# Moving a third of layer two's own-row projections from the second pass over the edges to the first, in a graph layer with a mixture of experts behind it

## The chip, the cores and the metric

The kernel runs on one core of a Trainium2 chip. The metric is the device time of one execution in microseconds; the times shown are the median, the lowest and the highest of several runs. A core has five engines with instruction streams of their own: TensorE (PE, with PEld for its weight loads), VectorE (DVE), ScalarE (ACT), GpSimd (POOL) and SyncE (SP, which here only issues DMAs). They meet through semaphores.

## The reference

The input is `x` (6250 x 512, f32) and 100000 edges `src`, `dst`, sorted by `dst`. Two graph layers run on the normalised rows, then a mixture of experts:

```python
def _sage_layer(h, src, dst, W_self, W_neigh, b, n_nodes):
    agg = segment_sum(h[src], dst, num_segments=n_nodes)
    deg = segment_sum(ones_like(dst), dst, num_segments=n_nodes)
    h_neigh = agg / maximum(deg, 1.0)[:, None]
    return relu(h @ W_self + h_neigh @ W_neigh + b)
...
h = _sage_layer(layernorm(x), src, dst, W_self1, W_neigh1, b1, n)
h = _sage_layer(h, src, dst, W_self2, W_neigh2, b2, n)
x = x + h
x = x + moe(layernorm(x))    # 8 experts, the best 2 of each row
```

All weights of the graph layers are 512 x 512. What matters here is layer two: it needs, of each row of layer one's result h1, the *neighbour part* h1 @ W_neigh2 (summed over the edges later) and the *own part* h1 @ W_self2 + b2. The own part is what the change moves.

## The kernel before

The rows form 49 tiles of 128 (the last has 106). After a first stage (normalising), two passes over the edges follow, both written by the helper `sums` (from L200), then a stage for the experts that is left over.

**A pass.** The edges are cut into 782 lists of 128. A pass has 197 steps; a step takes four lists. For every list GpSimd issues one indirect DMA that gathers 128 rows of 2 KB (L220) into a buffer of a ring: 16 buffers in the first pass (tile `rows_t`), 12 in the second (parts of `big`). VectorE builds one-hot masks for a step (L230, `hot`) two steps ahead. PE multiplies masks and gathered rows into a strip of sums (L248, tile `pa`, eight instructions a step). GpSimd's gathers run three steps ahead of PE in the first pass and two in the second; a gather must wait until PE has used up the buffer that it writes, which is that of four steps earlier in the first pass and three in the second. Three steps make a group: after each group the strip is rounded into three bf16 parts (L258, L272 to L274). When all groups of a tile of rows are there, `take_out` (L283) multiplies them with a selection (L290) and so gets the tile's sums. Tile 8 is taken out in step 40, tile 9 in step 43, tile 10 in step 49; this pattern, three tiles in twelve steps, goes on: for tile b with b mod 3 = 2 the next tile follows three steps later and the one after that six steps later.

**The first pass** ("first sums") calls `layer1` (L552) for each tile that is taken out. It schedules the tile's work in later steps, as (steps behind, place in the step, function):

- u0 (+1, "post", tiles below 36 only): the tile's own part of layer one, xn @ W_self1 (L559), with a bias add (L564);
- u1 (+1, "mid"): the sums are transposed (L194, evicted at L196);
- u2 (+2): times W_neigh1 (L559), then scaled and added to the own part by VectorE (L573, tile `h`);
- u3 (+3): h is transposed, with the relu in the eviction (L196), and for tiles below NS = 36 stored to DRAM as `h1T` (L578);
- u4 (+4): times W_neigh2, copied by ScalarE into part b of `big` (L584) and stored to `z2` (L585);
- u5 (+5, "post", tiles 36 to 44): times W_self2 (L559), bias add (L591), stored to `s2` (L592). For tiles 45 to 48 it is done after the pass.

"mid" is between the step's L248 matmuls and the closing of a group, "post" is at the step's end. A projection (L559) is four f32 matmuls of 128x512, which the profile shows as eight instructions. `big` (49 parts of 128x512) holds in turn each tile's transposed rows, its own part of layer one, and the z2 and s2 rows that are being stored; behind the stores, every fourth tile, SyncE loads 1 MB of the experts' first weights W1 into parts 0 to 31 (L609). W_self2, its bias and two padded copies of the edge lists are loaded from ScalarE's queue when tile 18 is taken out (L597 to L600).

**The second pass** ("second sums") gathers from `z2`. Beside its steps, `each` (L1021) gives out work. In three of every four steps, from step 1 to step 47, it calls `share_of(q)` (L921): tile q's h1T, which SyncE has fetched into a slot of three (L919), times W_self2 (L925, eight instructions), bias add (L927), store to `s2` (L928), and the fetch for tile q + 3. So the own parts of tiles 0 to 35 are made here: the "shares". `route` (L946), called for each tile that is taken out, adds the own part (fetched from s2 one tile ahead, L943) and the neighbour part (L1005), normalises, finds the experts and sends the rows to them by two indirect DMAs (L993). From about step 60 on, each even step also starts a tile of experts' work (L814 to L886). W2 is loaded by 1 MB in eight of the tiles (L640).

**The order.** In both passes the instructions of PE, DVE, ACT and POOL stand in the order in which the program writes them (`manual_schedule`); only SyncE's DMAs are ordered by the framework. All queues are worked in order: what stands behind a waiting instruction of the same engine waits too.

Of the kernel before, what the change touches and what calls it, by code (L numbers as in the profile page):

```python
# [39 lines left out]
P = 128  # L40
# [9 lines left out]
def bcast(ap, n):  # L50

    return bass.AP(tensor=ap.tensor, offset=ap.offset, ap=[[0, P], [1, n]])
# [15 lines left out]
def gnn_moe(ctx, tc, x, src, dst, Ws1, Wn1, gb1, Ws2, Wn2, gb2, Wg, W1, b1, W2, b2, gamma, beta, out):  # L68
    nc = tc.nc
# [7 lines left out]
    NB = (N + P - 1) // P  # L77
# [11 lines left out]
    s2 = dram.tile([N, D], F32, name="s2")  # L89
# [100 lines left out]
    def transposed(pool, psp, t, func, n=P, out=None, bufs=2):  # L190

        pt = psp.tile([P, C, P], F32, name="pt")
        for c in range(C):
            nc.tensor.transpose(pt[:, c, :n], t[:n, c * P : (c + 1) * P], ident[:n, :n])  # L194
        tT = pool.tile([P, C, P], F32, name="tT", bufs=bufs) if out is None else out
        nc.scalar.activation(tT[:, :, :n], pt[:, :, :n], func)  # L196
        return tT
# [128 lines left out]
    def part(i):  # L326
        return big[:, i * D : (i + 1) * D]
# [87 lines left out]
    NS = 3 * NB // 4  # L415
# [124 lines left out]
    lay = b_ctx.enter_context(tc.tile_pool(name="lay2", bufs=1, side="left"))  # L540
    wn2, ws2 = (lay.tile([P, C, D], F32, name=name) for name in ("wn2", "ws2"))
    bb2 = lay.tile([P, D], F32, name="bb2")
    h1T = dram.tile([NS, P, D], F32, name="h1T")

    with tc.tile_pool(name="s1", bufs=2, side="right") as pool, \
            tc.tile_pool(name="s1a", bufs=1, space=PSUM) as pap, \
            tc.tile_pool(name="s1p", bufs=2, space=PSUM) as psp:

        LATE = 4
        late = []  # L550

        def layer1(b, pa, pd):  # L552
            n = rows[b]
            r = slice(b * P, b * P + n)
            own = {}

            def project(ph, tT, w, start, stop):
                for c in range(C):
                    nc.tensor.matmul(ph, tT[:, c], w[:, c], start=(start and c == 0), stop=(stop and c == C - 1))  # L559

            def u0():
                ps = psp.tile([P, D], F32, name="pm")
                project(ps, xnT[b], ws1, True, True)
                nc.vector.tensor_add(part(b), ps, bb1)  # L564

            def u1():
                own["aT"] = transposed(pool, psp, own["a"], AF.Copy)

            def u2():
                ph = psp.tile([P, D], F32, name="pm")  # L570
                project(ph, own["aT"], wn1, True, True)
                own["h"] = pool.tile([P, D], F32, name="h", bufs=1)
                nc.vector.scalar_tensor_tensor(own["h"], ph, rcnt[:, b : b + 1], part(b), op0=OP.mult, op1=OP.add)  # L573

            def u3():
                own["hT"] = transposed(pool, psp, own["h"], AF.Relu, out=xnT[b] if b >= NB - LATE else None)
                if b < NS:
                    nc.sync.dma_start(h1T[b], own["hT"].rearrange("p c n -> p (c n)"))  # L578

            def u4():  # L580
                pz = psp.tile([P, D], F32, name="pm")
                project(pz, own["hT"], wn2, True, True)
                t = part(b if b < NB - LATE else b - LATE)
                nc.scalar.copy(t, pz)  # L584
                nc.sync.dma_start(z2[r], t[:n])  # L585

            def u5():
                ps = psp.tile([P, D], F32, name="pm")
                project(ps, own["hT"], ws2, True, True)
                t = part(b - 1 if b < NB - LATE else b)  # L590
                nc.vector.tensor_add(t, ps, bb2)  # L591
                nc.sync.dma_start(s2[r], t[:n])  # L592

            if b == 0:
                nc.scalar.dma_start(wn2, Wn2.rearrange("(c p) f -> p c f", p=P))
            if b == NS // 2:
                nc.scalar.dma_start(ws2, Ws2.rearrange("(c p) f -> p c f", p=P))  # L597
                nc.scalar.dma_start(bb2, bcast(gb2, D))
                nc.scalar.dma_start(dpad[:E], dst)
                nc.scalar.dma_start(spad[:E], src)  # L600
            nc.vector.tensor_reduce(deg[:, b : b + 1], pd[:, 0 : NDEG : NDEG // 2], AX.X, OP.add)
            nc.vector.tensor_scalar(rcnt[:, b : b + 1], deg[:, b : b + 1], 1.0, None, op0=OP.max)
            nc.vector.reciprocal(rcnt[:, b : b + 1], rcnt[:, b : b + 1])
            own["a"] = pool.tile([P, D], F32, name="a", bufs=1)
            nc.scalar.copy(own["a"], pa)
            e = (b - 5) // 4
            if b >= 5 and (b - 5) % 4 == 0 and e < NE:

                nc.sync.dma_start(w1[:, e * KD : (e + 1) * KD].rearrange("p (c h) -> p c h", c=C),  # L609
                                  W1[e].rearrange("(c p) h -> p c h", p=P))  # L610
            if b >= NB - LATE:
                late.append(u5)
            return ([(1, "post", u0)] if b < NS else []) + [
                (1, "mid", u1), (2, "mid", u2), (3, "mid", u3), (4, "mid", u4)
            ] + ([(5, "post", u5)] if NS <= b < NB - LATE else [])

        with tc.manual_schedule(engines=HAND):
            sums(xn_d, pool, pap, lambda: pap.tile([P, D], F32, name="ps"),
                 pap.tile([P, 2, NDEG], F32, name="pn"), layer1,
                 lambda: pool.tile([P, D], F32, name="rows_t", bufs=16), 16)  # L620
            for u5 in late:
                u5()
# [274 lines left out]
    def fetch_hidden(k):  # L897
        nc.sync.dma_start(part(NW + k % NE), hd[rest[k]])

    with tc.tile_pool(name="s2", bufs=2, side="right") as pool, \  # L900
# [13 lines left out]
        shares = {}  # L914

        def fetch_h1(q):
            if q < NS:
                shares[q] = w2[:, (21 + q % 3) * D : (22 + q % 3) * D]
                nc.sync.dma_start(shares[q], h1T[q])  # L919

        def share_of(q):  # L921
            hT = shares.pop(q).rearrange("p (c n) -> p c n", c=C)
            ps = psp.tile([P, D], F32, name="ph")
            for c in range(C):
                nc.tensor.matmul(ps, hT[:, c], ws2[:, c], start=(c == 0), stop=(c == C - 1))  # L925
            t = w2[:, (24 + q % 2) * D : (25 + q % 2) * D]
            nc.vector.tensor_add(t, ps, bb2)  # L927
            nc.sync.dma_start(s2[q * P : (q + 1) * P], t)  # L928
            fetch_h1(q + 3)
            if q == 0:  # L930
                fetch_own(0)
# [5 lines left out]
        def fetch_own(b):  # L937
            if b < NB:
                n = rows[b]
                xa = pool.tile([P, D], F32, name="xa")  # L940
                nc.sync.dma_start(xa[:n], x[b * P : b * P + n])
                sa = part(NW + 12)
                nc.sync.dma_start(sa[:n], s2[b * P : b * P + n])  # L943
                own[b] = xa, sa
# [76 lines left out]
        def each(i):  # L1021


            at_slot[0] = i
            if i == last_slot + 1:
                for k in range(EARLY):
                    fetch_hidden(k)
            q = i - 1 - i // 4
            if i % 4 and q < NS:
                return [(0, "post", lambda: share_of(q))]  # L1030
            j = up_next[0]
            if i % 2 or j >= upto_n[-1]:
                return []
            c = max(c for c in range(len(n0)) if n0[c] <= j)
            if ready.get(c, 1 << 30) > i:
                return []
            up_next[0] += 1
            u = Up(j, pool, psp, keep=j not in soon)
            todo = [(1, "post", u.fetch), (3, "mid", u.turn_x), (5, "mid", u.times), (6, "mid", u.turn_h)]
            if j in soon:  # L1040
                d = {}

                def begin():
                    d[0] = Down(j, u.hT, u.e, pool, psp, pool.tile([P, D], F32, name="y", bufs=1))
                    d[0].rows = {"gamma": "ph", "beta": "ph"}
                    d[0].times()

                todo += [(8, "mid", begin), (8, "post", lambda: d[0].spread()), (9, "mid", lambda: d[0].scale()),
                         (10, "post", lambda: (d[0].affine(), d[0].finish()))]
            return todo  # L1050

        for q in range(3):
            fetch_h1(q)
        with tc.manual_schedule(engines=HAND):
            sums(z2, pool, pap, lambda: psp.tile([P, D], F32, name="ph"), None, route, ring, 12, each)
# [316 lines left out]
```

## Time and profile before

| | us |
|---|---|
| median of 3 runs | 3350.38 |
| lowest, highest | 3343.76, 3356.97 |
| the profiled execution's own time | 3328.7 |
| its span, first to last instruction | 3326.4 |
| mean granted PE clock | 0.894 |
| first sums, first to last gather's matmul (L248, `rows_t`) | 121.3 to 1294.5 |
| second sums, the same (`big`) | 1336.2 to 2760.3 |
| shares (L925), first to last | 1354.6 to 1656.1 |

| engine | busy us | share of the span |
|---|---|---|
| PE | 2694.6 | 81% |
| POOL | 1846.9 | 56% |
| DVE | 1346.4 | 40% |
| ACT | 691.5 | 21% |

A line of a group reads: source line, engine, operation, what it writes <- what it reads, size, count | busy time, mean duration of one in ns | idle time of the engine just before, and what ended most of it. "issue" is time in which the engine waited for nothing that the profile shows, "remote" a semaphore whose sender is not found. PE's ends are modelled, its starts are measured. Busy shares are means over stages with different limits, and so the text goes by stage.

### The profile page before, as it was taken

To read this page: it belongs to the slowest core of one execution; us is meant where nothing else is said; L and a number is where in the kernel's file an instruction comes from. 1 tells how busy PE (TensorE), PEld (TensorE's weight loads), DVE (VectorE), ACT (ScalarE), POOL (GpSimd) and SP (SyncE) were. 2 spreads that over 40 slices of the span, in tenths; PEclk is the share of its full clock that TensorE was granted. 3 is DMA by queue.
4 is the path that set the end of the run, shared out by engine and by line. 5 is a ranking of instruction groups with operands and counts; after the bars stand their busy time and mean duration, and the time that the engine had idled before them with its cause. 6 is when DMAs were issued, how large, how long until landed. Compare 5 with 4: busy or idle time off the path is not lost. (4 is left out here: it accounts for less than half of the span.)

```text
span 3326.4 us, 34415 instructions
## 1 busy us (share of the span) xinstructions
PE 2694.6 (81%) x10010; PEld 1075.8 (32%) x10010; DVE 1346.4 (40%) x4313; ACT 691.5 (21%) x1261; POOL 1846.9 (56%) x2129
## 2 busy tenths in 40 slices
PE   6768878788887789778747888887888888899995
PEld 3223323233332333223212333332333333344442
DVE  6422222222222222234334454445445454654675
ACT  2211111111111111011112222232222322122221
POOL 4466666666666662666666555555655551650443
PEclk8988988988989899889868888997988998999997
DMA  7767667766776663888877667776766663321696
GB/s 234 229 193 211 205 205 211 226 208 206 217 210 207 198 200 107 268 270 283 269 237 259 220 206 218 221 221 210 222 206 209 216 219 109 129 73 57 217 305 226
DMA packets 266654, 693.41 MB, mean 208 GB/s; under 512 B 42684, under 2 KB 42798, under 8 KB 266428
## 3 DMA queue, kind: packets, MB, share of 16 engines
q0 software_dynamic: 144000, 464.43, 46.4%
q1 hardware_dynamic: 118796, 219.84, 19.2%
q10 hardware_dynamic: 3664, 6.85, 0.6%
q8 instruction: 85, 1.39, 0.2%
q14 instruction: 109, 0.89, 0.1%
HBM read 554.35 MB, written 137.40 MB: 208 GB/s over the span
## 5 line engine op out<-in xcount | busy, mean ns | idle before, releaser
L220 POOL DMA_INDIRECT big<-z,srcT x782 | 748.9, 958 | 584.2 <-PE pa L248 241.8
L220 POOL DMA_INDIRECT rows_t<-xn_d,srcT x782 | 740.5, 947 | 470.2 <-issue 187.5
L559 PE MATMUL pm<-wn,tT 128*128 128x512 f32 x752 | 365.9, 631 | 46.7 <-ACT tT L196 29.1
L826 PE MATMUL ph<-big,xg 128*128 x544 | 312.8, 727 | 79.1 <-DVE y L884 50.1
L860 PE MATMUL py<-w,hT 128*128 x656 | 306.7, 611 | 13.0 <-ACT y L878 8.5
L248 PE MATMUL pa<-big,hot 128*32 128x512 f32 x1564 | 252.0, 662 | 9.9 <-DMA big<-z,srcT 5.9
L248 PE MATMUL pa<-rows_t,hot 128*32 128x512 f32 x1564 | 238.8, 621 | 12.4 <-DMA rows_t<-xn_d,srcT 9.6
L1095 POOL DMA_INDIRECT big<-ys,yrow x98 | 106.9, 1090 | 230.6 <-DMA ys<-y 135.0
L559 PEld LDWEIGHTS pm<-wn,tT 128*128 128x128 f32 x752 | 142.2, 199 | 275.2 <-issue 214.8
L826 PEld LDWEIGHTS ph<-big,xg 128*128 128x128 f32 x544 | 121.5, 235 | 281.2 <-issue 214.2
L290 PE MATMUL ps<-st,sel 128*128 128x512 bf16 (+1 forms) x459 | 139.1, 450 | 47.7 <-issue 38.7
L860 PEld LDWEIGHTS py<-w,hT 128*128 128x128 f32 x656 | 119.3, 192 | 177.9 <-issue 135.9
L925 PE MATMUL ph<-w 128*128 128x512 f32 x288 | 148.8, 665 | 23.4 <-DVE big L1005 17.3
L559 PE MATMUL pm<-ws,big 128*128 128x512 f32 x320 | 153.9, 627 | 0.0
L993 POOL DMA_INDIRECT xs<-big,slot x98 | 98.6, 1006 | 98.1 <-DVE slot L989 43.1
L273 ACT CAST st<-pa 128x512 bf16<-128x512 f32 x132 | 77.3, 586 | 344.3 <-DVE pa L272 211.8
L265 DVE CAST counts<-pn 128x8 bf16<-128x8 f32 x66 | 10.9, 166 | 340.4 <-remote 177.0
L837 DVE TENSOR_SCALAR hT<-pt,b1T 128x128 f32<-128x128 f32 x272 | 76.7, 343 | 177.6 <-PE pt L834 133.0
L290 PEld LDWEIGHTS <-sel 128*128 128x128 bf16 (+1 forms) x918 | 85.7, 107 | 189.9 <-issue 96.5
L1005 DVE SCALAR_TENSOR_TENSOR big<-ph,rcnt,big 128x512 f32<-128x512 f32 (+1 forms) x49 | 36.8, 751 | 266.1 <-PE ph L290 94.0
L1136 PE MATMUL ph<-big,xg 128*128 x296 | 136.9, 605 | 0.0
L290 PE MATMUL ph<-st,sel 128*128 128x512 bf16 (+1 forms) x459 | 120.1, 411 | 17.5 <-DVE sel L280 14.6
(265 smaller groups left out, 3473.8 us busy)
## 6 DMA issues: line engine op xcount, KB each, us to landing
xg<-xs SPq DMA_DIRECT2D x105, 256.0 KB
ys<-y SPq DMA_DIRECT2D x105, 256.0 KB
rows_t<-xn_d,srcT POOLq DMA_INDIRECT x782
big<-z,srcT POOLq DMA_INDIRECT x782
z<-big SPq DMA_DIRECT2D x48, 256.0 KB
xa<-in_x SPq DMA_DIRECT2D x48, 256.0 KB
big<-s SPq DMA_DIRECT2D x48, 256.0 KB
accs<-xa SPq DMA_DIRECT2D x48, 256.0 KB
```

Source lines behind the costliest of these rows:

```text
L220: nc.gpsimd.indirect_dma_start(out=gathered[t], out_offset=None, in_=z[:, :], in_offset=bass.IndirectOffsetOnAxis(ap=srcT[:, t : t + 1], a ...
L248: nc.tensor.matmul(pa[0][q * SW : (q + 1) * SW], hots[i][:, q], gathered.pop(t), start=(j == 0), stop=(j == TS - 1 or t == NT_E - 1), tile ...
L273: nc.scalar.copy(st[1][:k], pa[:k])
L290: nc.tensor.matmul(ps, sel[:k], st[h][:k], start=(g == a and h == 0), stop=(g == z and h == 2))
L559: nc.tensor.matmul(ph, tT[:, c], w[:, c], start=(start and c == 0), stop=(stop and c == C - 1))
L826: nc.tensor.matmul(ph, self.xT[:, c], w1[:, bass.ds(self.e * KD + c * D, D)], start=(c == 0), stop=(c == C - 1))
L837: nc.vector.tensor_scalar(hT[:, c], pt[:, c], b1T[:, bass.ds(self.e * HC + c, 1)], 0.0, op0=OP.add, op1=OP.max)
L860: nc.tensor.matmul(self.py, self.hT[:, c], w2[:, bass.ds(self.e * KD + c * D, D)], start=(c == 0), stop=False)
L925: nc.tensor.matmul(ps, hT[:, c], ws2[:, c], start=(c == 0), stop=(c == C - 1))
L993: inst = nc.gpsimd.indirect_dma_start(out=xs[:, :], out_offset=bass.IndirectOffsetOnAxis(ap=slot[:n, b, k : k + 1], axis=0), in_=t["xn"][: ...
L1095: nc.gpsimd.indirect_dma_start(out=yk[:n], out_offset=None, in_=ys[: ready[0] * P, :], in_offset=bass.IndirectOffsetOnAxis(ap=yrow[:n, b, ...
L1136: nc.tensor.matmul(ph, u.xT[:, c], w1[:, bass.ds(u.e * KD + c * D, D)], start=(c == 0), stop=(c == C - 1))
```

## The change

The list `later` holds the tiles whose own part stays in the second sums: all below 6, and of 6 to 35 those whose number modulo 3 is not 2. The ten others (8, 11, ..., 35) get a u5 in the first sums, like the tiles 36 to 44, and no `h1T` store. Their s2 rows go through part b of `big`, where the z2 rows of the same tile were a step before; tiles from 36 on use part b - 1 as they did. W_self2 and what is loaded with it is loaded when tile 3 is taken out, not tile 18. In the second sums 26 shares are left, one in every odd step from 1 to 51.

```diff
+    later = [b for b in range(NS) if b < 6 or b % 3 != 2]
...
                 own["hT"] = transposed(pool, psp, own["h"], AF.Relu, out=xnT[b] if b >= NB - LATE else None)
-                if b < NS:
+                if b in later:
                     nc.sync.dma_start(h1T[b], own["hT"].rearrange("p c n -> p (c n)"))
...
                 project(ps, own["hT"], ws2, True, True)
-                t = part(b - 1 if b < NB - LATE else b)
+                t = part(b - 1 if NS <= b < NB - LATE else b)
                 nc.vector.tensor_add(t, ps, bb2)
                 nc.sync.dma_start(s2[r], t[:n])
...
-            if b == NS // 2:
+            if b == 3:
                 nc.scalar.dma_start(ws2, Ws2.rearrange("(c p) f -> p c f", p=P))
...
-            ] + ([(5, "post", u5)] if NS <= b < NB - LATE else [])
+            ] + ([(5, "post", u5)] if b < NB - LATE and b not in later else [])
...
         def fetch_h1(q):
-            if q < NS:
+            if q < len(later):
                 shares[q] = w2[:, (21 + q % 3) * D : (22 + q % 3) * D]
-                nc.sync.dma_start(shares[q], h1T[q])
+                nc.sync.dma_start(shares[q], h1T[later[q]])
...
-            nc.sync.dma_start(s2[q * P : (q + 1) * P], t)
+            nc.sync.dma_start(s2[later[q] * P : (later[q] + 1) * P], t)
...
-            q = i - 1 - i // 4
-            if i % 4 and q < NS:
+            q = i // 2
+            if i % 2 and q < len(later):
                 return [(0, "post", lambda: share_of(q))]
```

In the changed kernel the lines from L547 on stand two lines lower.

## The prediction

> **What bounds the kernel now.** I read the windows view first, one stretch for each stage, then the costliest groups of the page, then GpSimd's waits in the same stretches, and last the timeline of a few steps around the place where work is added. The windows (length, busy time and instructions of PE, PEld, DVE, ACT, POOL, then granted clock, DMA share, GB/s):
>
> ```profile
> 121.00:1276.00 1155.00, 924.81 (x3643) 346.66 (x3643) 285.89 (x880) 173.10 (x308) 735.20 (x778) 0.90 0.70 207
> 1336.00:1656.00 320.00, 247.97 (x900) 89.77 (x900) 113.45 (x374) 43.85 (x82) 207.14 (x233) 0.87 0.83 274
> 1656.00:1735.00 79.00, 42.85 (x182) 12.86 (x181) 25.35 (x91) 12.66 (x22) 54.10 (x62) 0.67 0.75 248
> ```
>
> The first row is the first sums, the second is the part of the second sums that holds the 36 shares, the third is the same sums just after the last share. In the first sums PE is busy 80% (924.81 of 1155). The groups give the unit prices:
>
> ```profile
> L220 POOL DMA_INDIRECT rows_t<-xn_d,srcT x782 | 740.5, 947 | 470.2 <-issue 187.5
> L559 PE MATMUL pm<-wn,tT 128*128 128x512 f32 x752 | 365.9, 631 | 46.7 <-ACT tT L196 29.1
> L925 PE MATMUL ph<-w 128*128 128x512 f32 x288 | 148.8, 665 | 23.4 <-DVE big L1005 17.3
> ```
>
> GpSimd issues a gather in 0.95 us and then pauses 0.30 us, so four gathers, one step, take at least 5.0 us, and 197 steps 985 us of the 1155. The rest is waiting. GpSimd's waits in the first sums (us, times, longest):
>
> ```profile
> POOL rows_t L220 <- issue: 186.9, 566, 4.8
> POOL rows_t L220 <- remote: 101.2, 83, 3.5
> POOL rows_t L220 <- PE pa L248: 98.1, 60, 4.6
> ```
>
> The first line is mostly the 0.30 us pauses; all other lines together are 233 us, 20% of the stage, and they are waits for PE to give a ring buffer back. So two things bound a step: GpSimd's 5.0 us, and PE's lateness. Where PE is late is seen by taking the first L248 matmul of every step as the step's start. Steps 37 to 156 repeat in twelves (three tiles in each), and the means of ten repeats, by step number modulo twelve, are, as duration / PE idle in it: 1: 8.1/3.1; 2: 8.7/2.8; 3: 5.2/0.4; 4: 9.1/4.2; 5: 8.7/0; 6: 5.4/0.6; 7: 3.6/0; 8: 8.8/0.4; 9: 5.4/0.6; 10: 1.6/0; 11: 6.5/1.4; 0: 0.9/0. The sum is 71.9 us, 6.0 a step, with 13.4 us of PE idle. From 5 to 10 PE works without a pause and GpSimd waits for it; at 1, 2 and 4 PE waits for ScalarE and VectorE, which wait for PE's own signals, that arrive late ("remote").
>
> The place of the change is step 9 (45, 57, ...). PE and POOL lines of steps 45 and 46:
>
> ```profile
> 409.09 1.06 PE L248 MATMUL pa<-rows_t,hot 128*32 128x512 f32 x8
> ...
> 410.09 3.70 PE L559 MATMUL pm<-wn,tT 128*128 128x512 f32 x8
> 410.41 0.94 POOL L220 DMA_INDIRECT rows_t<-xn_d,srcT  x1 [0.59 <-PE pa L248]
> ...
> 413.72 1.06 PE L248 MATMUL pa<-rows_t,hot 128*32 128x512 f32 x8
> ...
> 416.51 0.94 POOL L220 DMA_INDIRECT rows_t<-xn_d,srcT  x1 [1.40 <-PE pt L194]
> ```
>
> Step 45's matmuls end at 410.15 and the gather for step 49, which takes their buffers, starts 0.26 us later; the gather for step 50 likewise follows the matmuls of step 46. Over the ten repeats the gathers that use the buffers of step 9 start 0.4 us, and of step 10 0.7 us, after the matmuls' ends. GpSimd hangs on PE exactly here.
>
> **The change, part by part.** *Ten projections come into the first sums* (tiles 8, 11, ..., 35). The order of PE's instructions puts each between the u2 of the next tile and the L248 of step 10: in the timeline between the eight that start at 410.09 and the L248 at 413.72. One is eight instructions; at full clock eight take 3.70 us (410.09), and by the group 365.9/752 x 8 = 3.9 us. The L248 of step 10 moves back by 3.9 us, and with it the gather that follows it by 0.7 us, where the shortest such distance seen is 0.2; so 3.9 - 0.5 = 3.4 us are felt by GpSimd each time, 34 us in ten. Some comes back: steps 10, 11 and 0 are PE's lightest, and steps 1, 2 and 4 hold 10.1 us of PE idle. But this idle ends with signals that come when GpSimd has stopped and its transfers have drained, and GpSimd is what has been delayed; so I count a fifth as absorbed: **+27 us**. Bounds: 0 (all of it fits into the 13.4 us of idle) and 54 (ten at the 5.40 us that eight such instructions take at 753.85, after a pause).
>
> *VectorE* gets ten bias adds. The same kind of add takes 0.69 us (L564), 7 us in all, in an engine that is 25% busy. The add stands behind the h of the next tile (L573), so that chain is not held up; behind it stand the next one-hot masks (414.49), which wait until the projection ends, some 3.9 us later. They are for steps 48 and 49, and step 48 starts at 420.9, with the projection's delay on top. Nothing, while signals come in time; rival three prices the rest. The add also writes the buffer that tile's z2 row block is being stored from: a new wait for a DMA. That store is issued at 405.83 and the add could start at 417.4 at the earliest; the longest wait for such a store that SyncE's own waits show is 3.5 us, so 11.6 us cover it.
>
> *DMAs:* ten s2 stores take the place of ten h1T stores, 256 KB each, in the same stage; no byte more. In SyncE's queue each stands behind its tile's z2 store and ahead of the next tile's h1T store, and some W1 loads go behind an h1T store; W1 is used only in the second sums. The loads of Ws2, the bias and the two padded edge lists move from tile 18 to tile 3 in ScalarE's queue: 2.1 MB in the same stage, some 25 steps before the first use. Nothing.
>
> *Ten shares leave the second sums.* 80 PE instructions, 148.8/288 x 80 = 41 us of PE time, ten adds, ten loads and ten stores, 5.2 MB. What that brings is set by what bounds those steps. By the same step starts, steps 2 to 47 with three shares in four take 291.7 us, 6.48 each; steps 52 to 64, without any share, take 78.2 us, 6.52 each, though PE is busy 54% there instead of 77%. GpSimd's waits other than for issue are 59.6 of 320 us with shares and 13.1 of 79 us after, 18.6 and 16.6%. If the two points tell of a share's cost, 36 shares are worth 320 x (1 - 0.814/0.834) = 8 us at most, ten about 2. The stretch after the shares holds three W2 loads of 1 MB in twelve steps, more than the stretch before, so it flatters the shares; I take **-4 us**. Bounds: 0, and -41 (all of PE's time); the bytes alone, at the row's 274 GB/s, are 19 us.
>
> *Half the steps instead of three in four*, up to step 51 instead of 47: the last two shares now lie in steps 49 and 51, whose PE idle (2.3 and 7.8 us) takes most of them in. No tile's s2 is needed earlier than it comes: tile 9's is made in step 17 and read after step 40.
>
> The granted clock is 0.87 with shares and 0.67 without, and eight instructions take 3.70 us in a busy stretch and 5.40 us after a pause. The Trainium skill, TensorE: Matmul & The Clock Gate, Part 1: The HAM clock gate, states the rule behind such rows, that an idle window of about 3.4 us halves the clock until a busy one has passed; it speaks against the change, since the thinned steps leave PE idle more often, and it would charge the 26 remaining shares up to 26 x 1.7 = 44 us of PE time (an estimate) where the sum above charges none, because PE does not set those steps.
>
> **Sum:** +27 - 4 = +23 us. The profiled execution took 3328.7 us (span 3326.4), so that it would take 3351.7; the median of the runs shown is 3350.4, 21.7 us above the profiled one, so that I forecast **3373 us** for the median.
>
> **Rivals.** *One, no difference:* the 3.9 us disappear in the idle of steps 1, 2 and 4. For it: 10.1 us of idle stand there in every twelve steps, and an additional wait of GpSimd lets transfers drain, and so PE's late signals through, earlier. Against it: the gather hangs on L248 within 0.7 us. +6 - 4: 3352.
>
> *Two, faster:* shares are dearer in the second sums than in the first, because DMA is at 0.83 there against 0.70 and PE idles after them in stalls of 10 us and more (8.8 in step 14, 11.5 in step 38). If a stall goes with every third share that leaves, ten times 4.1 us of PE time or the 19 us of bytes come back: between the two -30, with +6 for the first sums, -24: 3326. Against it: 6.48 and 6.52 us a step.
>
> *Three, clearly slower:* VectorE, held at the new add by a late signal, builds masks too late, and PE waits for them. VectorE's waits for remote signals reach 14.6 and 26.0 us in this stage (deg and counts); if every new add waits 5 us past the masks' due time, that is 10 x 5 = 50 more: 3423. It decides from the point where the signal is over 7 us late (from 417.4 to 420.9 + 3.9).
>
> That the change doesn't do what it says can be left aside: the instruction order shows ten projections more in the first sums and ten shares fewer in the second.
>
> **How the numbers follow.** The forecast has 0.52, one 0.27, two 0.13, three 0.08. Under 0.5%, 17 us, a measurement of this kernel can't tell a change from none. The forecast's own range is +10 to +38; an eighth of it lies within 17 us. Slower: 0.52 x 0.88 + 0.08 = 0.54; faster: nearly all of two, 0.12; same: the rest, 0.34. The range leaves out half of two and most of three: 3332 to 3396.
>
> **What would show it.** Right: the step starts of the first sums show step 9 longer by 3.7 to 4 us, GpSimd's wait ahead of the gathers for step 2 grown by some 3 us, and the stage longer by 20 to 35 us; the second sums up to step 52 shorter by under 10 us. Wrong, by rival one: step 9 longer but step 1 or 2 shorter by as much. By two: the share stretch shorter by 20 us or more. By three: VectorE's wait at the new add over 7 us, and PE waiting for hot masks, which it hardly does now. The steps after 64 should not change at all.

## The result, and the profile after

| | before | after |
|---|---|---|
| median of 5 runs, us | 3350.38 | 3380.28 |
| lowest, highest | 3343.76, 3359.7 | 3376.29, 3389.74 |
| the profiled execution's own time | 3328.7 | 3380.28 |
| its span | 3326.4 | 3378.0 |

The ratio is 1.0104, with a 95% interval of 1.0073 to 1.0136: slower by 30 us at the median. The two profiles lie further apart, 51.6 us of span, because the one of before is 21.7 us under its median and the one of after is the median.

Where the 51.6 us are follows from the first L248 of each step: first gather's matmul +2.5 us; first sums 1173.1 -> 1207.5, +34.4 (steps 37 to 157: 722.4 -> 766.6, +44.2; the rest -9.8); between the passes 41.7 both; second sums to step 52 342.6 -> 349.6, +7.0, steps 52 to 64 -7.2, the rest +4.1; what comes after the passes +10.8, with the same work in both (in the profiles of the later runs this part takes 573 to 581 us with either kernel; 566.1 and 576.9 here). So most of the loss, 34.4 us, is in the first sums, and the second sums gave nothing back. There, steps 2 to 47 fell from 291.7 to 285.0 us, but steps 47 to 52, into which the last two shares were moved, grew from 26.5 to 37.6.

The same 120 steps (37 to 157) and the share stretch to step 52, by the windows view of before (length, busy time and instructions of PE, PEld, DVE, ACT, POOL, granted clock, DMA share, GB/s):

```profile
349.00:1072.00 723.00, 589.31 (x2368) 226.48 (x2364) 185.77 (x577) 114.13 (x203) 457.64 (x484) 0.90 0.70 211
...
1336.00:1679.00 343.00, 259.50 (x956) 93.00 (x959) 121.25 (x399) 46.02 (x85) 223.53 (x251) 0.87 0.82 270
```

and of after:

```profile
348.00:1115.00 767.00, 615.81 (x2418) 242.29 (x2440) 190.43 (x579) 112.52 (x201) 457.77 (x484) 0.90 0.66 196
...
1373.00:1723.00 350.00, 249.45 (x865) 84.86 (x879) 116.21 (x392) 47.52 (x88) 227.12 (x256) 0.83 0.78 254
```

In the first row PE gains 26.5 us of busy time (some matmul records of after are missing) and GpSimd none, but the stretch is 44 us longer, and DMA falls from 211 to 196 GB/s: the engines wait more. In the second row PE does 10 us less and DMA is less busy, and still the stretch is 7 us longer: the busy time of neither bound it.

The place of the change, steps 45 and 46, in the timeline of after:

```profile
406.30 1.07 PE L248 MATMUL pa<-rows_t,hot 128*32 128x512 f32 x8
...
408.15 3.70 PE L561 MATMUL pm<-wn,tT 128*128 128x512 f32 x8 [0.78 <-ACT tT L196]
...
411.69 3.60 PE L561 MATMUL pm<-ws,tT 128*128 128x512 f32 x8
411.89 0.75 DVE L575 SCALAR_TENSOR_TENSOR h<-pm,rcnt,big 128x512 f32<-128x512 f32 x1 [0.71 <-PE pm L561]
415.21 1.07 PE L248 MATMUL pa<-rows_t,hot 128*32 128x512 f32 x8
415.32 0.69 DVE L593 TENSOR_TENSOR big<-pm,bb 128x512 f32<-128x512 f32 x1 [2.68 <-PE pm L561]
...
418.01 0.95 POOL L220 DMA_INDIRECT rows_t<-xn_d,srcT  x1 [5.69 <-PE pa L248]
```

The added eight (411.69) stand between u2 and the L248 of step 46, which starts 8.9 us after that of step 45, not 4.6; and GpSimd stands for 5.69 us before it gathers for step 50. Over ten repeats of twelve steps, step 9 grew from 5.4 to 8.1 us, the wait ahead of the gathers for step 2 from 0.2 to 3.0 us, and the twelve steps from 71.9 to 76.3 us. (Such sums of twelve, the prediction's and all below, leave out step 156, the last of the stretch; with it the 120 steps give 72.2 and 76.7.) Steps 1, 2 and 4, whose PE idle was 3.1, 2.8 and 4.2 us, now have 0.7, 11.2 and 0.6: three stalls have become one long one.

What ends that long stall is ScalarE's copy of the taken-out sums, which by the program waits for a signal from PE. ScalarE's waits at this copy, in before:

```profile
ACT a L605 <- remote: 130.0, 17, 16.0
```

and in after:

```profile
ACT a L607 <- remote: 252.3, 29, 16.1
```

17 and 29 of 49 copies wait for a signal whose sender is not found, up to 16 us, long after PE's record of the matmuls. From the start of the last matmul of a take-out (L290) to this copy the median is 2.6 us in before and 4.2 us in after, the longest 14.2 and 14.5.

### The profile page after: what moved, and what is told of

Read it like the earlier page. It is cut to its first block, busy times and chain, and to the rows that moved or that the text cites. A ratio compares the mean times of both kernels' runs of the same rounds, so it can differ in the third digit from the quotient of the medians.

```text
span 3378.0 us, 34248 instructions
## 1 busy us (share of the span) xinstructions
PE 2702.9 (80%) x9914; PEld 1083.4 (32%) x10010; DVE 1347.7 (40%) x4313; ACT 690.1 (20%) x1261; POOL 1846.1 (55%) x2129
## 5 line engine op out<-in xcount | busy, mean ns | idle before, releaser
L248 PE MATMUL pa<-big,hot 128*32 128x512 f32 x1564 | 276.4, 671 | 31.1 <-issue 15.7
L248 PE MATMUL pa<-rows_t,hot 128*32 128x512 f32 x1564 | 241.4, 616 | 12.8 <-DMA rows_t<-xn_d,srcT 9.7
L194 PE MATMUL pt<-ident,a 128*128 128x128 f32 x196 | 36.6, 318 | 164.1 <-ACT a L607 136.1
L561 PE MATMUL pm<-ws,big 128*128 128x512 f32 x320 | 167.3, 673 | 0.0
L603 DVE TENSOR_REDUCE deg<-pn 128x1 f32<-128x2 f32 x49 | 7.8, 159 | 352.8 <-remote 274.9
L274 DVE TENSOR_TENSOR st<-pa,st 128x512 bf16<-128x512 f32 x132 | 91.2, 691 | 89.0 <-ACT st L273 47.8
L290 PEld LDWEIGHTS <-sel 128*128 128x128 bf16 (+1 forms) x918 | 80.6, 101 | 140.1 <-issue 57.7
L290 PE MATMUL ps<-st,sel 128*128 128x512 bf16 x411 | 106.8, 397 | 21.7 <-issue 19.7
```

What stands on the lines that cost most here:

```text
L248: nc.tensor.matmul(pa[0][q * SW : (q + 1) * SW], hots[i][:, q], gathered.pop(t), start=(j == 0), stop=(j == TS - 1 or t == NT_E - 1), tile ...
L274: nc.vector.tensor_sub(st[2][:k], pa[:k], st[1][:k])
L290: nc.tensor.matmul(ps, sel[:k], st[h][:k], start=(g == a and h == 0), stop=(g == z and h == 2))
```

## Experiments

Theory after this result: the ten projections delay PE where GpSimd's gathers hang on it, about 3.4 us each. Rivals: PE's time counts wherever it stands; the new add or store holds something; the signals that come late are the cause, and the change only meets them.

**First and second part, place, size.** e1, the added projections alone:

```diff
-            q = i // 2
-            if i % 2 and q < len(later):
+            q = i - 1 - i // 4
+            if i % 4 and q < NS:
...
-                nc.sync.dma_start(shares[q], h1T[later[q]])
+                nc.sync.dma_start(shares[q], h1T[q if q in later else q - 1])
```

> The first sums as in the changed kernel, with the ten added projections and ten fewer h1T stores; the second sums with the pattern of before, 36 shares in three steps of four. (Ten of these work on a neighbouring tile's h1T and go to a spare array, so that the work is the same and the output too.) If the whole loss lies in the first sums, as the prediction has it: the time of the changed kernel within 8 us, 30 us over before (1.009), and the profile's first sums 40 to 48 us longer than before's in steps 37 to 157. If the second sums gave something back that the profiled run hides: 10 to 20 us over the changed kernel.

e2, the thinned shares alone:

```diff
-            q = i - 1 - i // 4
-            if i % 4 and q < NS:
+            q = i // 2
+            if i % 2 and q < len(later):
...
-                    nc.sync.dma_start(h1T[b], own["hT"].rearrange("p c n -> p (c n)"))
+                    nc.sync.dma_start(h1T[b] if b in later else s2[r], own["hT"].rearrange("p c n -> p (c n)"))
```

> The first sums as before, with no added projection; the second sums as in the changed kernel, 26 shares, one in every odd step. (The own part of ten tiles is left out: in the first sums their transposed h goes to s2 in place of h1T, so that bytes and stores stay.) The prediction's size for the shares that leave is -4 us, and the two profiles show -4 us up to step 47 and +7 up to step 52: 0.996 to 1.002. Rival two of the prediction, shares dear in the second sums: -19 to -41 us, 0.988 to 0.994.

e3, the projections in the empty step:

```diff
-            ] + ([(5, "post", u5)] if b < NB - LATE and b not in later else [])
+            ] + ([(8 if b < NS else 5, "mid", u5)] if b < NB - LATE and b not in later else [])
```

> The changed kernel with the ten added projections three steps later, after the matmuls of the step that has no other work of layer one (48, 60, ...); the transposed h has three buffers in place of two for that. If the loss comes from the place, that is, from the delay of the matmuls on which GpSimd's next gather hangs: most of it goes, 0 to 12 us over before (1.000 to 1.004), and the wait ahead of the gathers for step 2 modulo twelve falls from 3.0 to under 1 us. If it comes from PE's time as such, wherever it stands: as the changed kernel, 25 to 45 us over before.

e4, a quarter of each projection:

```diff
-                project(ps, own["hT"], ws2, True, True)
+                project(ps, own["hT"], ws2, True, True, C if b >= NS else 1)
```

> The changed kernel with one of the four matmuls of each added projection (the three others left out, so the ten own parts are wrong); the bias add, its waits and the store stay. If the loss is the time by which PE's next gather-matmuls move back: PE delay 0.9 in place of 3.7 us, of which 0.5 is not felt, so 0 to 10 us over before. If it is the add with its wait for a late signal, or the store: 25 to 35 us over before, as the changed kernel.

| | median, us | ratio to before, 95% interval |
|---|---|---|
| before, same chip | 2974.74 | |
| e1, first part alone | 2979.03 | 1.0018 (1.0004 to 1.0032) |
| e2, second part alone | 2978.10 | 1.0007 (0.9989 to 1.0024) |
| e3, other place | 2980.56 | 1.0023 (1.0008 to 1.0038) |
| e4, a quarter | 2976.95 | 1.0015 (0.9997 to 1.0034) |

No difference between the four says anything of the first result, because the loss is not there: on their chip the kernel before takes 2975 us, not 3350, and e1, which has all of the added work, is 4 us over it, not 30. e2 lies in its expected range and rules out rival two here; the prediction's -4 us for the second sums is just outside its interval, which goes from -3 to +7 us. e1 and e3, 4 and 6 us slower, are just clear of no difference. The profiles show one thing that differs from the first comparison: from the last L290 to the copy the median is 0.47 us in all four, the longest 1.6.

**The same kernels on a chip with prompt signals.**

> The changed kernel itself, beside before on the same chip. The first four kernels ran on a chip on which before takes 2975 us, and in their profiles PE's signals come at once (from the last matmul of a take-out to ScalarE's copy of it 0.5 us), where the profiles of before and after have a median of 2.6 and 4.2 us and up to 14. If the loss is PE's late signals, lengthened by the change: on a chip with prompt signals 0 to 10 us over before (1.000 to 1.003), on one with late signals 25 to 45 us (1.008 to 1.013). If the loss is PE's time: 25 to 45 us on both.

> The kernel before, for its profile on this chip. With prompt signals: the first sums' twelve steps take 60 to 61 us, as in the run without the added projections, and no stall of all three of PE, VectorE and ScalarE over 3 us. With late signals: 71 to 73 us.

e5 is 2977.65 us against 2975.31, 1.0002 (0.9988 to 1.0017): no difference. Twelve steps take 60.3 us in e5 and 60.1 us in e6, and the 722.4 us of before for steps 37 to 157 are 604.6 us in e6. (The stalls of PE, VectorE and ScalarE together that e6 was not to show over 3 us are there twice, 3.2 and 3.7 us.) Windows of these steps, e6 (the kernel before):

```profile
340.00:944.00 604.00, 590.49 (x2362) 220.47 (x2355) 187.33 (x577) 112.35 (x201) 456.32 (x482) 0.99 0.81 251
```

and e5 (the changed kernel):

```profile
340.00:948.00 608.00, 602.44 (x2455) 231.48 (x2454) 194.11 (x587) 113.92 (x204) 458.78 (x485) 1.00 0.81 247
```

604 us for 120 steps is 5.03 us a step, GpSimd's own issue (four times 0.95 + 0.30). GpSimd's waits for the matmuls, from 121 to 1100 us, e6:

```profile
POOL rows_t L220 <- PE pa L248: 30.5, 98, 0.9
```

and e5:

```profile
POOL rows_t L220 <- PE pa L248: 30.3, 95, 1.3
```

Nearly all of these are the pauses of 0.30 us: the added projections make GpSimd wait no longer. PE's busy time contains waits for gathers here, since L248 matmuls whose rows come one gather at a time overlap less. The 960 of the 120 steps are busy for 171.7 us in e6 and 127.7 us in the profile of before. In e5 they are busy for 151.4 us, and PE's idle time falls from 14.9 to 7.2 us; that is how 3.7 us more work in twelve steps fit into 60 us that look full. The granted clock is 0.99, and was 0.90; with stalls put into the program on a chip with prompt signals (e9 below) it is 0.92, so that the lower clock need not be a cause. The take-out of the timeline of e6:

```profile
407.56 0.81 PE L290 MATMUL ps<-st,sel 128*128 128x512 bf16 x3
...
408.45 0.59 ACT L605 COPY a<-ps 128x512 f32<-128x512 f32 x1 [1.40 <-PE pn L292]
```

The copy starts as the last matmuls end (407.56 + 0.81). All waits of this copy in e6 are put down to PE itself, none to "remote". So the theory that PE's added time is felt as such, everywhere, falls; and "GpSimd hangs on PE" holds where signals are late and not where they are prompt.

**Price of the shares.**

e8, no shares at all:

```diff
-            if i % 4 and q < NS:
-                return [(0, "post", lambda: share_of(q))]
+            if i == 1:
+                return [(0, "post", lambda: fetch_own(0))]
```

> The kernel before without any share in the second sums. (The own parts of tiles 0 to 35 are left out: the first sums store the transposed h to s2 in place of h1T.) It prices the 36 shares: by the prediction's comparison of steps with and without shares 0 to 8 us under before in all; by rival two, 36 times 4 us of PE time or 69 us of bytes, 60 to 150 us under before.

2974.45 us, 0.9997 (0.9977 to 1.0017). All 36 shares, 149 us of PE time and 19 MB, cost nothing that can be measured (its interval goes from -7 to +5 us). There was nothing to gain in the second sums on this chip.

**Making results late.** No later run met late signals again, so lateness was put into the program, in the kernel before (e9), the changed one (e10), and the changed one with e3's place (e11).

```diff
             own["a"] = pool.tile([P, D], F32, name="a", bufs=1)
+            for _ in range(16 if b % 3 == 1 else 0):
+                nc.scalar.copy(own["a"], pa)
             nc.scalar.copy(own["a"], pa)
```

> The kernel before with one result of the first sums made late on purpose: ScalarE copies the taken-out sums of every third tile (numbers 1 modulo 3) seventeen times instead of once, so that PE gets them 16 x 0.6 = 9.6 us later, about as late as in the two profiles with late signals. If PE then stalls once in twelve steps, 60.1 us per twelve steps become 64 to 70, 50 to 120 us over before. If the ring and the steps' slack hide it: under 15 us.

> The changed kernel with the same late results. If a projection's 3.7 us are felt as soon as PE's lateness, and not GpSimd's issue, sets the steps: 20 to 45 us over the kernel before with the same late results, about the loss of the first comparison, in the first sums alone. If the late results by themselves are not what makes the added work felt, because GpSimd's own hold by late signals is needed too: 0 to 12 us over it.

> The changed kernel with the same late results and the added projections three steps later, in the step without other work of layer one. If the place counts (the delay of the matmuls on which the gather for step 2 modulo twelve hangs): 15 us or more under the changed kernel with late results, near the kernel before with them. If PE's time as such counts: within 8 us of the changed kernel with late results.

| | median, us | ratio to before, 95% interval | twelve steps, us | first sums, us |
|---|---|---|---|---|
| before, same chip | 2974.76 | | | |
| e9, before, late | 3058.00 | 1.0281 (1.0257 to 1.0305) | 66.0 | 1063.3 |
| e10, after, late | 3093.06 | 1.0384 (1.0349 to 1.0419) | 69.4 | 1097.7 |
| e11, other place, late | 3097.68 | 1.0406 (1.0381 to 1.0431) | 69.9 | 1105.2 |

e10 is 35 us over e9, of which 34.4 us are in the first sums: the size of the first comparison, 30 and 34.4. Step 2 takes 17 us with 9 us of PE idle in both, as in the changed kernel's first profile (18.9 and 11.2); the first profile of before had three shorter stalls in its place, so that e9 is not a copy of it. Step 9 grows from 4.6 to 8.1 us, and of GpSimd's waits only the one ahead of the gathers for step 2 grows by over 0.5 us, from 0.1 to 2.9. GpSimd's waits of e9 from 121 to 1100 us (us, times, longest):

```profile
POOL rows_t L220 <- PE pa L248: 88.6, 84, 3.6
```

and of e10:

```profile
POOL rows_t L220 <- PE pa L248: 119.7, 89, 4.8
```

31 us more; over the whole stage it is 101.0 and 136.1 us, 35 more, all of the stage's 34.4. The first expectation for e11 fails: in the empty step the projection costs as much, 4.6 us more at the median. The wait ahead of the gathers for step 2 is back at 0.1 us, but the one for step 7 grew from 2.2 to 5.7. With PE late by a stall in twelve steps, its time counts at both places that were tried.

**Taking GpSimd's lead away.**

```diff
-                 lambda: pool.tile([P, D], F32, name="rows_t", bufs=16), 16)
+                 lambda: pool.tile([P, D], F32, name="rows_t", bufs=12), 12)
```

> The kernel before with a ring of 12 buffers in the first sums in place of 16, so that GpSimd runs two steps ahead of PE, not three. With late signals a stall lasts until GpSimd has filled the ring and its transfers have drained: four gathers fewer, 5 us less in each of some ten to twenty stalls, 20 to 100 us under before. With prompt signals the ring only covers PE's uneven steps: 10 to 60 us over before. If the ring covers nothing at all: no change.

> The changed kernel with a ring of 12 buffers in the first sums in place of 16. It takes from GpSimd the four gathers by which it is ahead, so that its gathers hang on PE as they did where signals came late, but with prompt signals. Against the kernel before with 12 buffers (1.0031, 9 us over before on its chip): 15 to 35 us more if a gather that hangs on PE is enough to make the projection felt; 0 to 8 us more if it takes stalls by late signals.

e7 (before, 12 buffers): 2981.02 us, 1.0031 (1.0014 to 1.0048). e12 (after, 12 buffers): 3011.54 us, 1.0119 (1.0083 to 1.0155). The two ran on different chips, on which before takes 2975.31 and 2974.76 us, so the ratios can be set side by side: 30.5 us more, 23 of them in the first sums (994.2 and 1017.4 us). The four buffers cost the kernel before 6 us, a little less than the 10 to 60 expected, and the changed kernel 34. With prompt signals, a ring that is four buffers shorter makes the change as dear as late signals do: the gathers for step 1, which now use step 10's buffers, wait 2.6 us in e12 and not at all in e7. GpSimd's waits from 121 to 1100 us, e7:

```profile
POOL rows_t L220 <- PE pa L248: 47.2, 115, 2.6
```

and e12:

```profile
POOL rows_t L220 <- PE pa L248: 68.5, 119, 3.4
```

21 us more, nearly all of the stage's 23. The other use of e7, whether a shorter ring shortens stalls by late signals, could not be told, since it met no late signals.

No kernel of the study is faster than the one before.

## Why the prediction was right, and where its reasons were not

- *The ten projections, +27 us*: right in sign and place for the executions that were compared: +34.4 us in the first sums. The size is in part luck: the 120 steps that hold the projections grew by 44.2 us, more than the 34 that the sum has with nothing absorbed, and the steps around them, to which no projection was added, took 9.8 us less. The signs named for the first sums came: step 9 longer by 2.7 us (3.7 to 4 were expected; step 9 of before had held late signals too, undisturbed it goes from 4.6 to 8.1), the wait for step 2's gathers longer by 2.8 us.
- *"I count a fifth as absorbed"* is the step that failed. Nothing was absorbed: 4.4 us per twelve steps, 2.8 by GpSimd's wait, and PE idle in steps 1, 2 and 4 grew from 10.1 to 12.5 us in place of taking the projection in. The argument given against absorption (the idle ends only when GpSimd has stopped, and GpSimd is what is delayed) was the better one; that its transfers must also have drained holds in the two longest stalls of before's 120 steps and not in most of the shorter ones (the last section has one of each).
- *The shares, -4 us* with bounds 0 and -41: the measured value is nil on the chips with prompt signals (0.9997 without any share; 1.0007 with 26). In the first comparison the sign named for it, the second sums shorter up to step 52, did not come: they were 7.0 us longer. Steps 2 to 47 gave back 6.7 us, but steps 47 to 52 took 11.1 more. What failed there is the step by which PE's idle time in steps 49 and 51 takes the last two shares in; in the later profiles, too, steps 47 to 52 take 29 to 32 us with the shares where they were and 34 to 37 with the 26 thinned ones. Reading it off the pace of steps with and without shares was right, reading it off PE's 41 us or the 19 us of bytes would have been wrong.
- *The premise, that two things bound a step, GpSimd's 5.0 us and PE's lateness,* was read rightly from the profile, but the lateness was taken for the kernel's. It belonged to the circumstances of those executions: the same program takes 722 us for 120 steps there and 605 on another chip. The waits named "remote" were in the table, and the prediction used them as a given, without asking whether the next execution would have them. On the chip of e5, with prompt signals, rival one (no difference) is the result: 1.0002.
- *The place* was held to be what made it dear. e11 says no: where a late copy sets the pace, the empty step is as dear.
- *Rival three*: the new add's waits reach 3.0 us (by VectorE's waits of after), under the 7 from which it decides, and PE's waits for a hot mask come to 0.4 us in all. It did not happen. The other covers held as well: no wait for the z2 store shows at the add.
- *The clock rule*: the clock fell from 0.87 to 0.83 in the share stretch, in the direction of the rule (The Trainium skill, TensorE: Matmul & The Clock Gate, Part 1: The HAM clock gate), and no cost of it was found: on the chips with prompt signals it fell likewise, from 0.96 (e6) to 0.92 (e2), at a total of 1.0007.

What is shown: the added PE work costs nearly nothing while GpSimd leads by a full ring (e5, +2 us, interval -4 to +5), and 30 to 35 us when that lead is used up by a late copy (e10) or a shorter ring (e12). That the first comparison's loss has this cause is supported by its size and by step 9 and the wait for step 2 growing by like amounts; it was not tried there, since no later run had late signals of its own, and what made the signals late there stays open.

## What to carry to other kernels

When two engines are nearly balanced, a ring between them hides added work only as long as the lead is whole: look at how full the ring is where the work is put, not at the busy shares. Before work is moved out of a stage, price it by taking it out altogether; here it was free on the chip where that was tried, and so nothing could be won there by moving it. A wait whose sender the profile does not name may belong to the condition of an execution and not to the program; a forecast that rests on it should say what it would be without.

## What the runs showed of the hardware

The same kernel takes 3350 us in the first comparison and 2975 us on the three chips of the later runs, each within some 1% (whether the first ran on a fourth chip, or on one of these in another condition, isn't recorded). The difference goes with the delay of PE's signals: from the last matmul of a take-out to the copy that waits for it, median 0.47 us in the prompt executions and 2.6 us, up to 14.2, in the first profile. In the trace of before, PE's signals are recorded 0.7 to 2.8 us apart while GpSimd gathers (713.85, 714.57, 715.99, 718.78, 721.59), and then nine of them 0.04 us apart from 725.86 on, 3.1 us after GpSimd's last gather instruction ended, with 7 DMA packets started in the microsecond before. From 714.5 to 726.0 no engine but GpSimd works. In most of the shorter stalls such a burst comes while transfers still flow (at 1003.74, 2.3 us after the last gather, with 63 packets in the microsecond before), so that the transfers need not have drained. The two traces of the first comparison also lack records: before's has 2476 of PE's signals and 11488 of the DMAs' (eight semaphores), e6's of the same program 2992 and 28769. So these spacings are of the signals that were recorded, and that the recording, and not the chip, differed in those executions is a rival that no run here settles. Transfers themselves are no slower: the gathers' packets of 4 KB take a median of 159 ns in before and in e6. The Trainium skill, TensorE: Matmul & The Clock Gate, The cost: per-tile semaphore tail, gives a price of some 26 ns for each signal that PE sends after the other. The closest signals stand 0.03 to 0.04 us apart in e6, of that order; delays of up to 14 us are not. What makes the signals late stays open.
